# Values for the next image, one step sooner and loaded in fewer transfers

## The chip, the cores and the metric

The kernel runs on one core of a Trainium2 chip. The metric is the device time in microseconds of one execution, the median of several runs. Four compute engines work side by side, each in the order of its own instruction stream: TensorE (PE, matrix products), VectorE (DVE), ScalarE (ACT) and GpSimd (POOL). SyncE (SP) computes nothing here; it issues nearly all DMA transfers, one after the other, and a transfer that has to wait for something holds up every later one of the same stream. Engines wait for each other, and for transfers, through semaphores.

## The reference

The input x is 8 images of 256 channels and 64 x 64 pixels, in float32. Two layers are added to it in turn.

Layer 0 is `x = x + L0(group_norm(x))`: three 1x1 convolutions, a small network that makes a 3x3 kernel for every pixel and group of channels, and the weighted sum of shifted maps with that kernel.

Layer 1 is `x = x + L1(group_norm(x))`, and it is what the change touches. With y the normed map:

```python
q = conv1x1(y, Wq, bq) / 8;  k = conv1x1(y, Wk, bk);  v = conv1x1(y, Wv, bv)      # 4 heads of 64 channels
uk = unfold(pad(k, 3, mode="reflect"), 7);  uv = unfold(pad(v, 3, mode="reflect"), 7)
att = softmax(einsum("bdn,bdkn->bnk", q, uk + position), axis=-1)               # 49 neighbours of each pixel
out_att = einsum("bnk,bdkn->bdn", att, uv)
wts = softmax(einsum("oc,bchw->bohw", Wfc, y) in 9 branches)
out_conv = sum over branches of depthwise3x3(relu(depthwise3x3(y))) * wts
L1 = rate1 * out_att + rate2 * out_conv
```

The point to keep is the reflection: values beyond the edge of the image are copies of rows 1, 2 and 3 (and of columns 1, 2, 3) counted from that edge.

## The kernel before

**Bands and steps.** An image is worked in 8 bands (`NB`) of 8 rows (`R`). Layer 1 of band g is one turn of the main loop, made of 8 steps (`STEPS`): a half of the channels (`ct`) times four pairs of 8 x 8 query tiles (`m`). In the loop's numbering, bands run on over the images: g = 8 b + i for band i of image b. Layer 0 runs 12 bands ahead (`AHEAD`) in the same loop, so its work for the next image lies among the steps of this one. Before g = 0 there are 12 lead-in turns with layer 0 alone, whose steps are much shorter.

**One step.** A step scores a tile pair against its keys (L737), masks and exponentiates (L751, L759, L768), transposes the probabilities of the step before (L774, copied out at L776), multiplies transposed probabilities by values into the tile `small` (L786), and does two products of the dynamic weights, `pf` (L873), evicted by ACT with an exponential (L878). The products with the values are done in the even steps, for the two steps before.

**Who orders what.** The schedule is written out by hand. `beside(g, s)` gives two lists of work that lies beside the attention of step s: `mid` runs in the middle of the step, before its second `pf` product, and `end` at its end. `steer(g, s)`, at the head of a step, issues loads: rows of x for layer 0 (`xc`, `xs`, `xg`), neighbours of layer 0's maps (`x3q`, L389 to L397), and the next band's residual `xr` (L997). `after(n, f)` defers work by n places, six places to a step. The Tile framework adds the semaphores; it never reorders an engine's stream.

**Values.** The padded map of values has 70 rows, cut into 9 chunks of 8 rows: chunk 0 holds three reflected rows and rows 0 to 4; chunk 8 holds the last three true rows and three reflected ones; the chunks between are shifted by three rows against the bands. Each query tile of band i needs chunks i and i + 1. A chunk j is made in three moves:

- `values(b, j, half)` (L592) multiplies normed rows `yp` by `wv` in two halves; ACT copies the results to `vc` (L600), a tile with a single buffer.
- `store_values` sends `vc` to a DRAM buffer `vd` of 8 rows of 70 columns: two transfers for the inner columns (L616), and six, or twelve where the number of rows is odd (chunk 0), for the reflected columns (L621, L625).
- `value_tile(b, j, u)` loads tile u of the chunk, u = 0 to 3, into a buffer `vt` (L642). There are 11 such buffers, reused in turn. For an inner chunk a tile takes two transfers. For chunks 0 and 8 it takes eight: two for the run of true rows and two for each of the three reflected rows, which are read from their source rows.

The rows `yp` of a band are loaded by `load_rows` (L553 to L557) and normed in place on ACT by `normalise` (L562). `pf`, `pv`, `ptp` and other short results share a ring of four PSUM buffers, in the order in which they are asked for.

**The seam between two images.** Chunk i + 2 is made in band i of its own image at steps 4 and 5, stored at the end of step 5 and loaded at the end of step 7. The first two chunks of an image have no such place, so they are made in band 7 of the image before (for image 0, in the last lead-in turn). Chunk 0 is made at steps 4 and 5 and loaded at the end of step 7; chunk 1 is made at steps 6 and 7, stored at the end of step 7, and loaded in band 0 of its own image: tile 0 at the end of step 0, tile 1 at the end of step 1, tiles 2 and 3 at the end of step 2. PE reads the first of them at step 2. Chunk 8 is made at step 4 of band 6 and loaded at the end of its step 7. Rows of `yp` for the next image are loaded at the ends of steps 0 and 1 of band 7 and normed at the ends of steps 1, 2 and 3.

Of the kernel before, what the change touches and what calls it, by code (L numbers as in the profile page):

```python
# [23 lines left out]
R = 8  # L24
BAND = R * W
NB = H // R
# [21 lines left out]
PAD = KA // 2  # L48
WP = W + 2 * PAD
TQ = 8  # L50
# [3 lines left out]
KW = TQ + 2 * PAD  # L54
# [32 lines left out]
def conv_layers_kernel(ctx: ExitStack, tc: tile.TileContext, ins: dict, out: bass.AP):  # L87
    nc = tc.nc
# [121 lines left out]
    images = [Image() for b in range(B)]  # L210
# [348 lines left out]
    def normalise(b, i, ct):  # L559
        im = images[b]  # L560
        v = im.yp[i][:, ct, PAD if i == 0 else 0 : PAD + R if i == NB - 1 else RP]
        nc.scalar.activation(v, v, AF.Identity, bias=im.aff[:, ct, 1:2], scale=im.aff[:, ct, 0:1])  # L562
# [44 lines left out]
    def store_values(b, j):  # L607
# [9 lines left out]
        for d in range(1, PAD + 1):  # L617
            for to, c in ((PAD - d, d), (PAD + W - 1 + d, W - 1 - d)):
# [3 lines left out]
                else:  # L622
                    for p in range(2):
                        o = vd[at + p : at + p + 2 * count[p] - 1 : 2, to : to + 1].rearrange("u c n -> c u n")
                        nc.sync.dma_start(out=o, in_=vc[p * W + c : p * W + c + 1, : count[p]])  # L625

    def value_tile(b, j, u):


        im = images[b]  # L630
        vd = im.vd[j]
        vt = im.vt[j, u] = w1.tile([CHUNK, 2, C], F32, tag="vt", name=f"vt_{b}_{j}_{u}", bufs=11)
        if j == 0:
            runs = [(PAD, PAD, R - PAD)] + [(PAD - d, PAD + d, 1) for d in range(1, PAD + 1)]
        elif j < NB:
            runs = [(0, 0, R)]
        else:
            runs = [(0, 1, PAD)] + [(PAD - 1 + d, PAD - d, 1) for d in range(1, PAD + 1)]
        for to, at, n in runs:
            for g in range(2):  # L640
                c0 = (2 * u + g) * TQ
                nc.sync.dma_start(  # L642
                    out=vt[to * KW : (to + n) * KW, g], in_=vd[at : at + n, c0 : c0 + KW]
                )

    def new_keys(i):

# [3 lines left out]
    def position(b, i):  # L651

        first, last = new_keys(i)
        n, a = last - first, i * R + first
        pe = images[b].pe[i] = w1.tile([P, KW - PAD, W], F32, tag="pe", name=f"pe_{b}_{i}", bufs=1)
        nc.gpsimd.tensor_add(
            pe[:, :n],
            pecol.unsqueeze(1).to_broadcast([P, n, W]),
            perow[:, a : a + n].unsqueeze(2).to_broadcast([P, n, W]),
        )  # L660

    def queries(b, i, ct):

        im = images[b]
        nm = f"{b}_{i}_{ct}"
        kb = im.kb[i, ct] = w1.tile([P, KW, WP], F32, tag="kb", name=f"kb_{nm}", bufs=3)
        if i:
            nc.gpsimd.tensor_copy(kb[:, : 2 * PAD], im.kb[i - 1, ct][:, R:])
        qb = im.qb[i, ct] = w1.tile([P, NT, TQ, TQ], F32, tag="qb", name=f"qb_{nm}")
        pq = ps.tile([P, R, W], F32, tag="gen", name=f"pq_{nm}", bufs=4)  # L670
        for kt in range(NCT):
            nc.tensor.matmul(  # L672
                pq, wq[:, kt, ct * P : (ct + 1) * P], im.yp[i][:, kt, PAD : PAD + R],
                start=(kt == 0), stop=(kt == NCT - 1),
            )
        nc.scalar.activation(
            qb.rearrange("p t r c -> p r t c"), pq.rearrange("p r (t c) -> p r t c", c=TQ),
            AF.Identity, bias=bq[:, ct : ct + 1], scale=HD**-0.5,
        )

    def keys(b, i, ct):


        im = images[b]
        first, last = new_keys(i)
        kb, pe = im.kb[i, ct], im.pe[i]
        bk = chan[:, ct, CBK : CBK + 1]
        pieces = []
        for a in range(first, last, R):
            n = min(R, last - a)  # L690
            pk = ps.tile([P, R, W], F32, tag="gen", name=f"pk_{b}_{i}_{ct}_{a}", bufs=4)
            for kt in range(NCT):
                nc.tensor.matmul(
                    pk[:, :n], wk[:, kt, ct * P : (ct + 1) * P], im.yp[i][:, kt, a : a + n],
                    start=(kt == 0), stop=(kt == NCT - 1),
                )
            pieces.append((a, n, pk))

        def finish():
            for a, n, pk in pieces:  # L700
                nc.vector.scalar_tensor_tensor(
                    kb[:, a : a + n, PAD : PAD + W], pk[:, :n], bk, pe[:, a - first : a - first + n],
                    ALU.add, ALU.add,
                )

                for d in range(1, PAD + 1):
                    src = (W, n), (W - 1 - 2 * d, 2)
                    nc.vector.scalar_tensor_tensor(  # L708
                        strided(kb, a * WP + PAD - d, (WP, n), (W - 1 + 2 * d, 2)), strided(pk, d, *src), bk,
                        strided(pe, (a - first) * W + d, *src), ALU.add, ALU.add,  # L710
                    )
            if i in (0, NB - 1):
                after(2, reflect)

        def reflect():
            for d in range(1, PAD + 1):
                to, at = (PAD - d, PAD + d) if i == 0 else (last - 1 + d, last - 1 - d)
                nc.scalar.copy(kb[:, to], kb[:, at])

        return finish  # L720
# [73 lines left out]
    def small_tile(nm):  # L794

        return ps.tile([P, 4 * P], F32, tag="small", name=f"small_{nm}")
# [117 lines left out]
    def beside(g, s):  # L914

        b, i = divmod(g, NB)
        bn, inx = divmod(g + 1, NB)
        mid, end = [], []

        early = i in (0, NB - 1)  # L920
        if g >= 0:
            if s == 2 - early:
                mid.append(lambda: queries(b, i, 1))
            if s == 3 - early:
                mid.append(lambda: keys(b, i, 1))
        early = inx in (0, NB - 1)
        if 0 <= g + 1 < B * NB:
            if s == 5 - early:
                mid.append(lambda: position(bn, inx))
            if s == 6 - early:  # L930
                mid.append(lambda: queries(bn, inx, 0))
            if s == 7 - early:
                mid.append(lambda: keys(bn, inx, 0))

        made = [(b, i + 2, 4)] if g >= 0 and i < NB - 1 else []
        if i == NB - 1 and 0 <= b + 1 < B:
            made = [(b + 1, 0, 4), (b + 1, 1, 6)]
        for bb, j, d in made:
            if s in (d, d + 1) and (j < NB or s == d):
                mid.append(lambda bb=bb, j=j, d=d: values(bb, j, s - d))  # L940
            if s == d + 1:
                end.append(lambda bb=bb, j=j: store_values(bb, j))
            if s == 7 and d == 4:
                for u in range(NT // 2):
                    end.append(lambda bb=bb, j=j, u=u: value_tile(bb, j, u))
        if g >= 0 and i == 0 and s in (0, 1, 2):
            for u in {0: (0,), 1: (1,), 2: (2, 3)}[s]:
                end.append(lambda u=u: value_tile(b, 1, u))

        nxt = [(b, i + 2, 0)] if g >= 0 and i + 2 < NB else []  # L950
        if i == NB - 1 and 0 <= b + 1 < B:
            nxt = [(b + 1, 0, 0), (b + 1, 1, 1)]
        for bb, ii, d in nxt:
            if s == d:
                end.append(lambda bb=bb, ii=ii: load_rows(bb, ii))
            if s in (d + 1, d + 2):
                end.append(lambda bb=bb, ii=ii, d=d: normalise(bb, ii, s - d - 1))

        alone = g < 0
        if 0 <= g + AHEAD < B * NB:  # L960
            bq_, iq = divmod(g + AHEAD, NB)
            if alone and s == 0:
                mid.append(lambda: small_maps(bq_, iq, small_tile(f"{bq_}_{iq}"))())
            if s == (2 if alone else 0):
                (mid if alone else end).append(lambda: value_maps(bq_, iq, 0))
            if s == (3 if alone else 1):
                mid.append(lambda: value_maps(bq_, iq, 1))
        if 0 <= g + AHEAD - 1 < B * NB and s == (2 if alone else 1):
            bh, ih = divmod(g + AHEAD - 1, NB)

            def hidden():
                parts = hidden_maps(bh, ih, alone)
                if not alone:
                    convs.extend(parts)

            end.append(hidden)
        if 0 <= g + AHEAD - 2 < B * NB and s in TAPS_AT[g < -1]:
            u = TAPS_AT[g < -1].index(s)
            end.append(
                lambda: tap_weights(*divmod(g + AHEAD - 2, NB), u, g < -1, PRODUCTS_AT[g < -1][u])  # L980
            )
        return mid, end
# [24 lines left out]
    with tc.manual_schedule():  # L1007
# [21 lines left out]
        for g in range(-AHEAD, B * NB):  # L1029
            b, i = divmod(g, NB)  # L1030
            for s in range(STEPS):
                ct, m = divmod(s, NT // 2)
                mid, end = beside(g, s)
                steer(g, s)
                if g >= 0:
# [146 lines left out]
```

## Time and profile before

| what | us |
|---|---|
| median of 3 runs (4012.72 to 4017.47) | 4012.74 |
| the profiled execution, as timed | 4010.67 |
| its span in the profile | 4008.9 |
| first scores of image 0 (end of the lead-in) | 246.3 |
| PE busy / DVE / POOL / ACT | 3807.0 / 3419.8 / 3174.8 / 2839.5 |

The page of a profile gives the busy time of each engine, its busy share over the span in 40 slices, and the costliest groups of instructions by line. The wait list says which engine stood still, until what, for how long in total, how many times, and the longest of them. A timeline row has the start, the length, the engine, the line, the operation, the tile written and those read, and in brackets the idle time before it with what ended it. A windows row has the length of a stretch, the busy time of each engine in it, the granted share of the TensorE clock, the busy share of the DMA engines, and the rate. "SPq" is SP's issuing of a transfer, not the transfer.

### The profile page before, as it was taken

The page shows a single profiled execution, that of the slowest core. Times are in us where ns is not written, and L with a number is a line of the kernel's source. Part 1 is how long each engine was busy: PE and PEld are TensorE (multiplying, and loading weights), DVE is VectorE, ACT ScalarE, POOL GpSimd, SP SyncE. Part 2 cuts the span into 40 slices and gives each one's busy share as a digit, 9 for nine tenths or more (in the row PEclk, how much of TensorE's full clock was granted, in tenths as well). Part 3 has the DMA queues.
Part 4 walks back from the last instruction along what each step waited for, and adds up shares of the span by engine and source line. Part 5 has one row for each costly group of instructions (what it writes and reads, how often), then busy time and mean ns, then how long its engine had stood idle before and what let it go on. Part 6 is the DMA issues. An engine that isn't in the chain of part 4 may idle for free.

```text
span 4008.9 us, 72420 instructions
## 1 busy us (share of the span) xinstructions
PE 3807.0 (95%) x24620; PEld 2116.9 (53%) x24620; DVE 3419.8 (85%) x7143; ACT 2839.5 (71%) x6779; POOL 3174.8 (79%) x2156
## 2 busy tenths in 40 slices
PE   6879999999999999999999999999999999999998
PEld 3445555555555555555555555555555555555554
DVE  5868988888888988888988888978988889977888
ACT  3457777677676777777777677777777677676776
POOL 4758988788987988878887888978888888965665
PEclk9989999999999999999999999999999999999999
DMA  8864543544444443444443544444443544322220
GB/s 230 201 165 113 134 114 104 136 125 113 127 115 122 124 124 101 125 132 120 124 115 104 138 125 118 110 130 124 118 115 90 129 116 104 85 61 88 71 65 32
DMA packets 493171, 469.42 MB, mean 117 GB/s; under 512 B 68432, under 2 KB 394624, under 8 KB 492544
## 3 DMA queue, kind: packets, MB, share of 16 engines
q1 hardware_dynamic: 489472, 460.23, 43.4%
q10 hardware_dynamic: 3328, 4.55, 0.3%
q8 instruction: 195, 3.19, 0.3%
q14 instruction: 176, 1.44, 0.1%
HBM read 325.64 MB, written 138.99 MB: 116 GB/s over the span
## 4 chain that ended last, share of the span: by engine, by line
PE 27%; POOL 26%; DVE 22%; ACT 10%; issue 7%; DMA 5%; SPq 3%; POOLq 0%; DVEq 0%; ACTq 0%
PE pf L873 13%; POOL xg L487 13%; POOL ex L1080 6%; DVE prod L479 5%; DVE acc L856 5%; DVE rec L894 4%; PE small L786 3%; ACT x L343 3%; PE sco L737 2%; PE ptp L774 2%; ACT ex L878 2%; DVE prob L751 2%; DMA x3q<-x 2%; PE pq L672 2%; DVE acc L830 2%
## 5 line engine op out<-in xcount | busy, mean ns | idle before, releaser
L873 PE MATMUL pf<-yp,c_wfc 128*128 128x512 f32 x4096 | 1917.1, 597 | 6.2 <-ACT ex L878 5.1
L487 POOL TENSOR_TENSOR xg<-xg,prod 128x1024 f32<-128x1024 f32 x549 | 1200.7, 2187 | 177.2 <-DVE prod L479 148.3
L873 PEld LDWEIGHTS pf<-yp,c_wfc 128*128 128x128 f32 x4096 | 744.0, 191 | 730.3 <-issue 647.1
L1080 POOL TENSOR_TENSOR ex<-ex,ex 128x1024 f32<-128x1024 f32 x384 | 907.9, 2364 | 55.9 <-ACT ex L878 51.8
L479 DVE SCALAR_TENSOR_TENSOR prod<-pw,c_par,x3q 128x1040 f32<-128x1040 f32 x576 | 737.9, 1288 | 124.8 <-PE pw L466 56.1
L830 DVE SCALAR_TENSOR_TENSOR acc<-yp,c_chan,acc 128x504 f32<-128x504 f32 (+3 forms) x1104 | 775.0, 702 | 50.7 <-ACT acc L821 30.3
L856 DVE SCALAR_TENSOR_TENSOR acc<-hid,c_chan,acc 128x504 f32<-128x504 f32 (+3 forms) x1024 | 749.8, 732 | 18.1
L878 ACT ACTIVATE ex<-pf 128x512 f32<-128x512 f32 x1024 | 602.1, 588 | 204.2 <-PE pf L873 184.3
L759 ACT ACTIVATE prob<-prob,nmax 128x196 f32<-128x196 f32 x1024 | 459.2, 451 | 217.1 <-DVE nmax L751 216.9
L768 ACT ACTIVATE prob<-prob,tot 128x196 f32<-128x196 f32 x1024 | 413.0, 452 | 235.3 <-DVE tot L766 235.1
L895 POOL TENSOR_TENSOR tot<-tot,rec 128x256 f32<-128x256 f32 x254 | 185.4, 730 | 412.9 <-DVE rec L894 387.9
L894 DVE RECIPROCAL rec<-tot 128x256 f32<-128x256 f32 x256 | 445.9, 1742 | 17.2 <-POOL tot L889 12.3
L776 ACT COPY pt<-ptp 112x512 f32<-112x512 f32 x511 | 294.8, 577 | 123.4 <-PE ptp L774 122.3
L751 DVE CUSTOM_DVE_ANT_0 prob<-sco,c_mask 128x196 f32<-128x196 f32 x1024 | 324.5, 354 | 20.4 <-PE sco L737 20.2
L786 PE MATMUL small<-pt,vt 112*64 112x64 f32 x8144 | 300.3, 226 | 37.5 <-DMA vt<-vd 37.1
L774 PEld LDWEIGHTS ptp<-ident,prob 128*112 128x112 f32 x2044 | 228.1, 134 | 188.9 <-issue 135.2
L774 PE MATMUL ptp<-ident,prob 128*112 128x128 f32 x2044 | 322.9, 281 | 1.3 <-ACT vc L600 1.3
L786 PEld LDWEIGHTS small<-pt,vt 112*64 112x64 f32 x8144 | 261.5, 138 | 116.7 <-issue 75.4
L737 PE MATMUL sco<-kb,qb 64*64 64x196 f32 x4096 | 236.1, 343 | 39.6 <-DVE kb L708 32.9
L592 PE MATMUL pv<-c_wv,yp 128*128 128x256 f32 (+1 forms) x1056 | 252.8, 382 | 2.6 <-ACT ex L878 2.1
L369 PE MATMUL p<-xc,w3s 128*128 128x512 f32 x512 | 248.4, 609 | 7.0 <-ACT ex L878 7.0
L466 PEld LDWEIGHTS pw<-h2n,c_c 128*128 128x128 f32 x1152 | 173.3, 191 | 153.5 <-issue 113.1
(139 smaller groups left out, 4756.9 us busy)
## 6 DMA issues: line engine op xcount, KB each, us to landing
vt<-vd SPq DMA_DIRECT2D x448, 112.0 KB
x<-x3n SPq DMA_DIRECT2D x128, 264.0 KB
x3q<-x SPq DMA_DIRECT2D x128, 264.0 KB
xc<-in_x SPq DMA_DIRECT2D x64, 512.0 KB
xg<-in_x SPq DMA_DIRECT2D x256, 128.0 KB
x<-xg SPq DMA_DIRECT2D x256, 128.0 KB
yp<-x SPq DMA_DIRECT2D x128, 256.0 KB
xr<-x SPq DMA_DIRECT2D x64, 512.0 KB
```

The lines of the kernel that those rows point to most:

```text
L479: nc.vector.scalar_tensor_tensor(prod[:, :, :RUN], pw[:, j, :RUN].unsqueeze(1).to_broadcast([P, SHARE, RUN]), par[:, PCB2 + k : PCB2 + k + 1],
L487: nc.gpsimd.tensor_add(im.xg[i], im.xg[i], rows(prod))
L759: nc.scalar.activation(prob[:, h, :NKEY], prob[:, h, :NKEY], AF.Exp, bias=nmax[:, h : h + 1], scale=-1.0, accum_out=tot[:, h : h + 1],)
L768: nc.scalar.activation(prob[:, h, :NKEY], prob[:, h, :NKEY], AF.Copy, scale=tot[:, h : h + 1])
L774: nc.tensor.transpose(ptp[:, h, ch], prob[:, h, ch * CHUNK : (ch + 1) * CHUNK], ident)
L786: nc.tensor.matmul(po[half[h], :, t * TQ : (t + 1) * TQ], im.vt[i + ch, m][:n, t, (2 * ct + h) * HD : (2 * ct + h + 1) * HD], pt[:n, h, ch ...
L830: nc.vector.scalar_tensor_tensor(o, yp[:, ct, ra + dr : rb + dr, ca + dc : cb + dc], chan[:, ct, CW1 + k : CW1 + k + 1], o, ALU.mult, ALU.add,
L856: nc.vector.scalar_tensor_tensor(o, hid[:, ra + dr : rb + dr, ca + dc : cb + dc], chan[:, ct, CW2 + k : CW2 + k + 1], o, ALU.mult, ALU.add,)
L873: nc.tensor.matmul(pf, wfc[:, kt, 2 * m + j, ct * P : (ct + 1) * P], images[b].yp[i][:, kt, PAD : PAD + R], start=(kt == 0), stop=(kt == N ...
L878: nc.scalar.activation(ex[:, j].rearrange("p (r c) -> p r c", r=R), pf, AF.Exp)
L894: nc.vector.reciprocal(rec, v)
L1080: after(4, lambda ex=ex, exb=exb: nc.gpsimd.tensor_add(ex, ex, exb))
```

## The change

Three things, in `value_tile`, a new `mirror_rows`, and `beside`:

- The reflected rows of chunks 0 and 8 are written into `vd` itself by three copies from DRAM to DRAM, one step after the chunk's store. A tile of these chunks is then loaded like any other, in two transfers.
- In band 7 (and the last lead-in turn) chunk 0 is made at steps 3 and 4, chunk 1 at steps 5 and 6, each one step sooner, with its store. Chunk 0 is still loaded at the end of step 7.
- Chunk 1's tiles are loaded in the middle of a step: 0 and 1 in step 0 of band 0, 2 and 3 in step 2.

Per image 48 fewer tile loads are issued (120 to 72) and 6 more copies.

```diff
+    def mirror_rows(b, j):
+        vd = images[b].vd[j]
+        for d in range(1, PAD + 1):
+            to, at = (PAD - d, PAD + d) if j == 0 else (PAD + d, PAD - d)
+            nc.sync.dma_start(out=vd[to], in_=vd[at])
+
     def value_tile(b, j, u):
         im = images[b]
         vd = im.vd[j]
         vt = im.vt[j, u] = w1.tile([CHUNK, 2, C], F32, tag="vt", name=f"vt_{b}_{j}_{u}", bufs=11)
-        if j == 0:
-            runs = [(PAD, PAD, R - PAD)] + [(PAD - d, PAD + d, 1) for d in range(1, PAD + 1)]
-        elif j < NB:
-            runs = [(0, 0, R)]
-        else:
-            runs = [(0, 1, PAD)] + [(PAD - 1 + d, PAD - d, 1) for d in range(1, PAD + 1)]
-        for to, at, n in runs:
-            for g in range(2):
-                c0 = (2 * u + g) * TQ
-                nc.sync.dma_start(
-                    out=vt[to * KW : (to + n) * KW, g], in_=vd[at : at + n, c0 : c0 + KW]
-                )
+        at, n = (0, R) if j < NB else (1, 2 * PAD)
+        for g in range(2):
+            c0 = (2 * u + g) * TQ
+            nc.sync.dma_start(out=vt[: n * KW, g], in_=vd[at : at + n, c0 : c0 + KW])
...
         made = [(b, i + 2, 4)] if g >= 0 and i < NB - 1 else []
         if i == NB - 1 and 0 <= b + 1 < B:
-            made = [(b + 1, 0, 4), (b + 1, 1, 6)]
+            made = [(b + 1, 0, 3), (b + 1, 1, 5)]
         for bb, j, d in made:
             if s in (d, d + 1) and (j < NB or s == d):
                 mid.append(lambda bb=bb, j=j, d=d: values(bb, j, s - d))
             if s == d + 1:
                 end.append(lambda bb=bb, j=j: store_values(bb, j))
-            if s == 7 and d == 4:
+            if s == d + 2 and j in (0, NB):
+                end.append(lambda bb=bb, j=j: mirror_rows(bb, j))
+            if s == 7 and j != 1:
                 for u in range(NT // 2):
                     end.append(lambda bb=bb, j=j, u=u: value_tile(bb, j, u))
-        if g >= 0 and i == 0 and s in (0, 1, 2):
-            for u in {0: (0,), 1: (1,), 2: (2, 3)}[s]:
-                end.append(lambda u=u: value_tile(b, 1, u))
+        if g >= 0 and i == 0 and s in (0, 2):
+            for u in (s, s + 1):
+                mid.append(lambda u=u: value_tile(b, 1, u))
```

## The prediction

> **What bounds the kernel now.** I read the page first: busy shares, then the slices.
>
> ```profile
> PE 3807.0 (95%) x24620; PEld 2116.9 (53%) x24620; DVE 3419.8 (85%) x7143; ACT 2839.5 (71%) x6779; POOL 3174.8 (79%) x2156
> PE   6879999999999999999999999999999999999998
> ```
>
> PE is at 9 in every slice after the lead-in, so from the first attention band on (246 us) only two things cost time: PE's work, and what makes PE stop. So the next view is the list of waits, PE's rows of it, and one of ACT's:
>
> ```profile
> PE small L786 <- DMA vt<-vd: 37.1, 15, 8.0
> PE sco L737 <- DVE kb L708: 32.9, 58, 1.3
> ACT vc L600 <- DMA vd<-vc: 16.5, 6, 11.9
> ```
>
> PE's longest wait is for value tiles: 37.1 us in 15 stops. In windows of one image each it comes once per image, in band 0 at step 2: 8.9 us in image 0, then 2.9, 4.1, 4.1, 5.1, 3.5, 2.6 and 5.8 (28.1 in images 1 to 7). The second row is 58 short stops all over the kernel, not near the change. The timelines of PE and of SP's queue show the stop of image 1:
>
> ```profile
> 751.90 0.80 PE L786 MATMUL small<-pt,vt 112*64 112x64 f32 x20
> 755.32 0.55 PE L786 MATMUL small<-pt,vt 112*64 112x64 f32 x8 [2.61 <-DMA vt<-vd]
> 756.17 0.34 PE L786 MATMUL small<-pt,vt 112*64 112x64 f32 x4 [0.30 <-DMA vt<-vd]
> 756.92 3.17 PE L873 MATMUL pf<-yp,c_wfc 128*128 128x512 f32 x4
> ```
> ```profile
> 716.57 1.26 SPq L616 DMA_DIRECT2D vd<-vc  x2
> 717.88 7.87 SPq L625 DMA_DIRECT2D vd<-vc  x12
> ...
> 729.30 17.12 SPq L642 DMA_DIRECT2D vt<-vd  x32
> 746.53 1.33 SPq L616 DMA_DIRECT2D vd<-vc  x2
> 747.90 3.83 SPq L621 DMA_DIRECT2D vd<-vc  x6
> 752.41 1.44 SPq L642 DMA_DIRECT2D vt<-vd  x2
> ```
>
> SP issues back to back for 25 us. The 32 loads of chunk 0 hold it for 17.12 us, chunk 1's store waits behind them to 746.53, its first tile goes out at 752.41 and PE, which asked for it at about 752.3, gets it at 755.3. The transfer is not slow, its issue is late. The stop costs more than its length: four pf matmuls took 3.17 us where the same group takes 1.88. The windows view (next to last: granted clock) says why:
>
> ```profile
> 751.06:770.15 19.09, 15.59 (x90) 8.49 (x89) 13.48 (x30) 10.53 (x25) 12.28 (x8) 0.91 0.52 166
> 757.40:760.70 3.30, 3.30 (x5) 1.27 (x4) 2.25 (x3) 2.38 (x4) 2.19 (x2) 0.50 0.92 323
> ```
>
> After the stop the clock is half for about 3.4 us. And ACT, in the same place, waits for rows of band 2 that SP issued only at 753.93:
>
> ```profile
> 758.32 1.14 ACT L562 ACTIVATE yp<-yp,aff 128x896 f32<-128x896 f32 x1 [5.79 <-DMA yp<-x]
> ```
>
> [...] in seven 19 us stretches, one for each stop of images 1 to 7, the clock is 0.91 (four) or 0.82 (three). [...] the copies wait for the stores, the tile loads for the copies. [...] A reflected row is 70 x 256 floats, 71.7 KB, and in the built program is a 16 x 1120 copy[...]. No trace here shows a DRAM to DRAM copy.
>
> **The change, part by part.**
>
> *Eight loads for 32, three copies.* For chunks 0 and 8 of each image, SP loses 24 issues and gains 3. In the trace 32 loads take 17.12 us; full-height loads take 4.49 us for 6, so 8 take 6.0. Three copies at the 0.5 of a small load are 1.6. Net 9.5 us of SP per chunk. SP time costs nothing by itself; it moves what is behind it. The copies' latency is unseen: from below 1.3 us (last store issued 725.75, ACT released 727.06), from above, if one ran at the 117 GB/s mean of the page, 2 us more each; I take landed 3 us after issue. Step 7 asks for it over 8 us after the copies, so it hides; it would show only beyond some 13 us.
>
> *One step sooner.* Matmuls of values (pv) move from steps 4 to 7 of band 7 to steps 3 to 6. PE's total is the same. At step 3, pv would come to PE at 698.05; its rows' second half is normalised by ACT from 696.97 for about 1 us, so the wait is 0 to 0.3 us. pv (1.72 us) then falls into a stop that PE has there anyway (1.02 us at 700.95, for a PSUM buffer): taken as zero. Steps 6 and 7 lose the 1.72 us, with POOL busy 15.76 of their 15.99 us; POOL's slack is in the next two steps (7.27 of 17.3).
>
> *SP's new order around image 1.* Chunk 0's second copy is out of ACT by about 711.5 (step 4 is at 709.5, and 1.7 later by step 3's longer work). Stores 9.2 us: 720.7. xr and x3q, moved behind them, 5.7: 726.4 (first used after 750). Copies: 728.0. Chunk 1's store 5.2: 733.2. xs and x1, 3.3: 736.5. Eight loads: 742.5. Tiles 0 and 1 of chunk 1, now at mid step 0 (buffers free at 735.7), 3.0: 745.5. Against 752.41 the first of them goes 9.9 us sooner and lands by 747, 5 us before PE asks. Rows of band 2 go at 745.5 in place of 753.93, landing about 750.5; ACT asks at 752.5. So both late transfers are in time; tiles 2 and 3 go at about 753, due at 766.
>
> *What it adds.* vc has one buffer: ACT may write chunk 1 into it only when chunk 0's stores have landed. In the trace ACT waits 0.87 us for that. In the new place stores land at 722.0 and ACT comes at about 717.5, since steps 4 and 5 are shorter than 5 and 6 with their double key matmuls: 4.5 us of wait. Behind it on ACT stand the evictions of pf and ptp. PE can go on while the ring of four PSUM buffers holds: pf of step 6 needs the buffer of this pv, at 722.2, free at 722.5. So 0.3 us is what I can derive, 1 us with what follows on DVE and POOL; bounds 0 and 3.5. Times 7: 7 us.
>
> **The sum.** Images 1 to 6: band 0 lasts 66.8, 69.4, 67.2, 68.8, 67.3, 66.4 us, first scores matmul to first scores matmul, 405.9 in all. Less stop and half clock (1.7 us at 0.91, 3.4 at 0.82) they leave 62.2, 63.6, 61.4, 60.3, 60.4, 62.1: the longer the stop, the more the other engines caught up in it. Without any stop I take 62.2 for all: 405.9 - 373.2 = 32.7. Image 7: 5.8 + 3.4 = 9.2, taken as 8.5. Image 0: SP does the same in short lead-in steps; ACT stands 11.87 us for vc there, store and first scores come 4 to 5 us sooner, and the last needed tile lands at about 265.6 in place of 275.3: 10. Less 7. Together 44. The profiled execution is 4010.7 (span 4008.9), so 3966.5; it is 2 us under the median, so 3968 against 4012.7.
>
> **The rivals.**
> - *All of it comes back*: the vc wait stays inside the ring, and ACT without its 5.8 us wait loses no catching up: 28.1 + 17.0 (clock) + 12 = 57, 3956. For: the 0.3 us above. Against: ACT-ended stops of 0.6 to 1.3 us in bands 7 and 0.
> - *The wait moves*: ACT's 4.5 us reaches PE as 3.5 us and brings its own half clock, 1.7: 5.2 in place of 1 in seven images, 29 us of the 44 lost: 3997.
> - *Slower*: the same vc wait, if SP comes to the stores late. To undo 44 us each image must lose 7.3, 1.7 of it clock, 5.6 idle; with the ring's 4 that is an ACT wait of 10 us, stores starting 6 us after 711.5. With 8 us more it is 4030. For: image 0's 11.87. Against: SP is idle from 704.3 in the trace.
> - *Nothing*: another late transfer takes the place of the tiles (rows of band 2 have 2 us, xs about 2.5): PE stops as before, 4008.
>
> **How the numbers follow.** Forecast 0.68, all 0.12, moved 0.11, slower 0.05, nothing 0.04. The range 3950 to 3998 takes in the first three with the vc bounds (0 to 3.5 us). 0.2% (8 us) is about what a measurement of this kernel can tell. Faster 0.90, same 0.04, slower 0.06.
>
> **What would show it.** Right: no wait of PE for vt in images 1 to 7, clock 1.00 in band 0, band 0 at 61 to 63 us, SP's run of L642 at step 7 about 6 us, ACT's wait for vc at 3 to 5 us per image, band 7 at 63 to 65. Wrong: PE still waiting for vt (SP not freed), pv waiting for yp at step 3, or pf waiting for ACT over 2 us in band 7.

## The result and the profile after

| | before | after |
|---|---|---|
| median, us | 4012.73 (4 runs, 4010.49 to 4017.47) | 3962.82 (4 runs, 3955.92 to 3964.21) |
| the profiled execution, timed / its span | 4010.67 / 4008.9 | 3964.1 / 3962.3 |

The ratio is 0.9869 [0.9854, 0.9885]: faster by 49.9 us, where 44 were forecast. The page after opens with nearly the same busy times; what went is PE's stopping, not its work:

```profile
PE 3794.8 (96%) x24620; PEld 2110.4 (53%) x24620; DVE 3418.4 (86%) x7143; ACT 2839.8 (72%) x6779; POOL 3174.4 (80%) x2156
```

The list of waits after, PE's line for value tiles and ACT's two for transfers (us in total, times, longest):

```profile
PE small L785 <- DMA vt<-vd: 1.7, 2, 1.3
```
```profile
ACT vc L600 <- DMA vd<-vc: 24.0, 6, 7.4
ACT yp L562 <- DMA yp<-x: 10.8, 4, 5.7
```

PE's 37.1 us for tiles are down to two stops in image 0. ACT's wait for rows (`yp`) is down from 63.7 us to 10.8. The wait that the change adds, for `vc`, is there: the list has it up from 16.5 to 24.0, and image by image it is 3.2 to 5.0 us ahead of images 1 to 7 (for two of them the profile names PE as what ended it). PE's timeline at step 2 of band 0 of image 1, after:

```profile
752.66 1.15 PE L785 MATMUL small<-pt,vt 112*64 112x64 f32 x32
...
754.23 1.88 PE L872 MATMUL pf<-yp,c_wfc 128*128 128x512 f32 x4
```

The 32 products run in one piece, and `pf` behind them takes 1.88 us in place of 3.17. The windows view of the same 19 us stretch has the clock (the third number from the end) at full speed:

```profile
751.06:770.15 19.09, 18.85 (x165) 11.28 (x164) 16.80 (x37) 13.20 (x30) 16.87 (x10) 1.00 0.55 167
```

SP's timeline over the same seam (each row a run of issues of one line):

```profile
711.19 1.29 SPq L616 DMA_DIRECT2D vd<-vc  x2
712.53 7.88 SPq L625 DMA_DIRECT2D vd<-vc  x12
...
724.81 2.11 SPq L632 DMA_DIRECT2D vd<-vd  x3
729.96 1.30 SPq L616 DMA_DIRECT2D vd<-vc  x2
731.30 4.14 SPq L621 DMA_DIRECT2D vd<-vc  x6
...
738.75 8.85 SPq L643 DMA_DIRECT2D vt<-vd  x12
747.70 0.40 SPq L553 DMA_DIRECT2D yp<-x  x1
```

The 12 loads at 738.75 are eight of chunk 0 and four of chunk 1. At 0.74 us each, the first tile of chunk 1 goes out at about 744.7 (forecast 742.5; before, 752.41), and PE asks for it at about 753.3. The rows of band 2 go at 747.70 (forecast 745.5; before, 753.93). ACT, after:

```profile
721.79 0.59 ACT L600 COPY vc<-pv 128x512 f32<-128x512 f32 x1 [3.46 <-DMA vd<-vc]
...
753.21 1.12 ACT L562 ACTIVATE yp<-yp,aff 128x896 f32<-128x896 f32 x1
```

The new wait is 3.46 us; the old one for rows (5.79 us) is gone.

**Where the time came from.** Bands are measured as in the prediction, first scores to first scores; "image 0" runs from the last small maps of the lead-in (L328) to band 1.

| stretch | before, us | after, us | difference | forecast |
|---|---|---|---|---|
| lead-in, to its last small maps | 212.8 | 216.8 | +4.0 | |
| image 0 | 106.2 | 103.1 | -3.0 | -10 |
| band 0 of images 1 to 6 | 67.64 on average | 61.03 | -39.7 in all | -32.7 |
| band 0 of image 7 | 58.50 | 50.25 | -8.2 | -8.5 |
| band 7 of images 0 to 5 (the vc wait) | 63.46 on average | 63.54 | +0.5 in all | +7 over seven images |

These add up to 46.4 of the 46.6 us by which the spans differ. The other 24 loads saved per image, those of chunk 8 at the end of band 6, bought nothing: bands 1 to 6 take 2734.8 us in all before and 2734.7 after, and band 7, which uses chunk 8, is no shorter. No reordering by the change explains the lead-in's part: the two traces drift apart by 2 us and more from about 130 us on, and every engine does the same work in the same order in both until 218. The place lies between 212 and 217 us in the twelve kernels run here. The two that keep the 32 loads have the two lowest values; why stays open.

### The profile page after: what moved, and what is told of

It reads as the page before. It is cut to its first block, busy times and chain, and to the rows that moved or that the text cites. A ratio compares the mean times of both kernels' runs of the same rounds, so it can differ in the third digit from the quotient of the medians.

```text
span 3962.3 us, 71885 instructions
## 1 busy us (share of the span) xinstructions
PE 3794.8 (96%) x24620; PEld 2110.4 (53%) x24620; DVE 3418.4 (86%) x7143; ACT 2839.8 (72%) x6779; POOL 3174.4 (80%) x2156
## 4 chain that ended last, share of the span: by engine, by line
PE 33%; POOL 26%; DVE 19%; ACT 9%; issue 6%; DMA 4%; SPq 3%; POOLq 0%; DVEq 0%; ACTq 0%
PE pf L872 15%; POOL xg L487 13%; POOL ex L1081 6%; DVE prod L479 4%; DVE rec L893 4%; DVE acc L855 4%; PE small L785 3%; ACT x L343 3%; PE sco L736 3%; PE ptp L773 2%; PE pq L671 2%; PE pk L692 2%; ACT ex L877 2%; POOL tot L888 2%; PE pv L592 2%
## 5 line engine op out<-in xcount | busy, mean ns | idle before, releaser
L736 PE MATMUL sco<-kb,qb 64*64 64x196 f32 x4096 | 235.9, 343 | 35.5 <-DVE kb L707 32.7
L888 POOL TENSOR_SCALAR tot<-tot 128x512 f32<-128x512 f32 x127 | 243.6, 1918 | 11.1
```

## The experiments

Four kernels make a square of the fewer loads and the earlier step. The third part of the change, the place of chunk 1's loads within a step, is the old one in both kernels that leave something out; E7 tests it.

| | old steps | one step sooner |
|---|---|---|
| 32 loads of chunk 0 | 4012.7 (before) | 4033.3 (E2) |
| 8 loads and 3 copies | 3958.2 (E1) | 3962.8 (after) |

**E1, fewer loads alone** (edit against the changed kernel):

```diff
-            made = [(b + 1, 0, 3), (b + 1, 1, 5)]
+            made = [(b + 1, 0, 4), (b + 1, 1, 6)]
...
-        if g >= 0 and i == 0 and s in (0, 2):
-            for u in (s, s + 1):
-                mid.append(lambda u=u: value_tile(b, 1, u))
+        if g >= 0 and i == 0 and s in (0, 1, 2):
+            for u in {0: (0,), 1: (1,), 2: (2, 3)}[s]:
+                end.append(lambda u=u: value_tile(b, 1, u))
```

> Only the reflected-row copies and the eight loads; values made at steps 4 to 7 as before, and chunk 1's tiles loaded at the ends of steps 0, 1 and 2 as before. Theory 1 (SP's 17 us of issues at step 7 made the tiles late): SP ends chunk 0's loads near 738 us instead of 746.4 around image 1, chunk 1's first tile goes at about 743 to 745 and lands by 748, before PE asks at 752. So no stop in images 1 to 7, band 0 at 61 to 62 us, and 3960 to 3968 in all: all of the gain from this part. ACT's wait for vc stays under 1 us. Rival (the step sooner is what brings the tiles in time): chunk 1 is stored too late without it, PE still waits 2 us or more per image with its half clock, and the time is 3990 to 4010.

Measured: 3958.21 us (4 runs, 3956.64 to 3960.37), just below the 3960 to 3968 expected; ratio to before 0.9865 [0.9849, 0.9882]. On SP's timeline of this kernel the loads of chunk 0 and the first tile of chunk 1 are

```profile
726.30 5.75 SPq L643 DMA_DIRECT2D vt<-vd  x8
...
738.22 1.41 SPq L643 DMA_DIRECT2D vt<-vd  x2
```

and PE, which comes to the products at 745.59 in this run, doesn't stop (it does in image 0, for 1.9 us). Band 0 of images 1 to 6 is 61.36 us, at full clock. So the whole gain comes with the fewer loads. The earlier step adds 0.33 us per image (61.36 to 61.03), 2 us over six images, and loses more than that in image 0, whose band 0 is 64.6 us here and 68.3 in the changed kernel.

What the 32 loads held up was SP, not the DMA engines. The windows view of the kernel before, over the 17.1 us in which it issues them, has the DMA engines busy for a share of 0.26 (the last number but one):

```profile
729.30:746.40 17.10, 16.34 (x101) 9.08 (x100) 13.54 (x36) 13.46 (x35) 10.91 (x10) 1.00 0.26 73
```

**E2, one step sooner alone** (against the kernel before):

```diff
-            made = [(b + 1, 0, 4), (b + 1, 1, 6)]
+            made = [(b + 1, 0, 3), (b + 1, 1, 5)]
...
-            if s == 7 and d == 4:
+            if s == 7 and j != 1:
```

> Only the step sooner for chunks 0 and 1, with their stores; 32 loads for chunks 0 and 8 and chunk 1's tiles at the ends of steps 0, 1 and 2, as before. Theory 1: SP does the same issues, with xr, x3q and now chunk 1's store (5 us) ahead of the 32 loads, so these end near 756 us around image 1 instead of 746.4 and the first tile of chunk 1 lands at 759: PE stops 6 to 8 us per image, the clock is half for 3.4 to 6.8 us after it, band 0 at 70 to 72 us, 4035 to 4060 in all. Rival (the step sooner brings the tiles in time): PE's stop shrinks or goes and the time is 3965 to 4000.

Measured: 4033.34 us (4 runs, 4032.48 to 4038.01), ratio 1.0054 [1.0039, 1.0069]: slower, if by a little less than the 4035 to 4060 expected. SP's timeline and PE's around image 1:

```profile
743.53 18.42 SPq L642 DMA_DIRECT2D vt<-vd  x34
```
```profile
763.52 1.27 PE L786 MATMUL small<-pt,vt 112*64 112x64 f32 x12 [6.03 <-DMA vt<-vd]
764.73 1.10 PE L774 MATMUL ptp<-ident,prob 128*112 128x128 f32 x4
765.62 3.62 PE L873 MATMUL pf<-yp,c_wfc 128*128 128x512 f32 x4
```

Chunk 1's store now stands ahead of the 32 loads on SP and waits for its values, so the loads begin at 743.53 in place of 729.30. Its first tile, the last two of these 34 issues, goes out at about 760.5 (before, 752.41). PE stops for 6 us, the clock is at 0.50 for 10.2 us around it, and band 0 of images 1 to 6 is 69.8 us on average.

**E3 and E8, the loads of chunk 0 issued three times and twice** in the changed kernel, into the same tiles (the values are the same, and SP's time grows). The loads of `value_tile` are split off as `load_tile`; E3 adds the lines below behind the first loads, E8 the same with `for u in range(NT // 2)`:

```diff
+                if j == 0:
+                    for u in 2 * list(range(NT // 2)):
+                        end.append(lambda bb=bb, u=u: load_tile(bb, 0, u))
```

> The changed kernel, with chunk 0's eight loads issued three times over (16 more issues at the end of step 7, about 11.5 us of SP). Theory 1: the slack of about 5 us that the tiles of chunk 1 have is used up, the first of them goes near 756 us around image 1 and lands at 758.5, so PE stops 5 to 7 us at step 2 of band 0, then runs 3.4 or 6.8 us at half clock; band 0 at 68 to 72 us, 4012 to 4045 in all. The half clock's price is read from it: 1.7 or 3.4 us beside the stop. Rival (transfers, not issues, set the time): 1.8 MB more per image would show as a busy share of the DMA engines near 1 and late rows everywhere; otherwise under 10 us in all.

> The changed kernel, with chunk 0's eight loads issued twice (8 more issues, about 5.8 us of SP). Theory: chunk 1's first tile goes near 750.5 us around image 1 and lands by 753, as PE asks: the slack is just used up, stop of 0 to 1 us per image, no half clock, band 0 at 61 to 62.5 us; rows of band 2 come 3 to 5 us late to ACT. Rival (slack smaller than 5 us): stops of 2 us or more, half clock, band 0 over 64 us.

Measured: E3 4042.35 us (4 runs, 4041.47 to 4042.83), ratio 1.0074 [1.0059, 1.0089], band 0 of images 1 to 6 71.0 us. E8, one execution: 3999.26 us, band 0 65.5 us. E8's PE and ACT around image 1:

```profile
757.20 1.09 PE L789 MATMUL small<-pt,vt 112*64 112x64 f32 x12 [1.82 <-DMA vt<-vd]
```
```profile
761.16 1.13 ACT L562 ACTIVATE yp<-yp,aff 128x896 f32<-128x896 f32 x1 [5.97 <-DMA yp<-x]
```

Nothing but more loads brings all of the old loss back, and more. The rival named for E3, that transfers and not their issue set the time, would have the DMA engines near full: while SP issues E3's 28 loads (745.9 to 765.6) their share is 0.51. Eight more loads are some 5.7 us; PE stopped for 1.2 on average, so tiles had about 4.5 us to spare (forecast 5). But band 0 is 4.5 us longer than 61.0, with stops for tiles of 1.2, where 61 to 62.5 were expected; and half clock, of which none was expected, follows in images 1, 3 and 7. More is at work than tiles. The second row shows a candidate: rows of band 2 come late too.

**E6, copies as late as possible**, at step 7 just ahead of the loads that read them:

```diff
-            if s == d + 2 and j in (0, NB):
+            if s == 7 and j in (0, NB):
```

> The changed kernel, with the three DRAM to DRAM copies issued at the end of step 7, right ahead of the tile loads that read them, instead of one step after the store. The gap on SP between the last copy and the first tile load is the copy's landing time. Theory: 1.5 to 3 us, so tiles go out 2 to 4 us later than in the changed kernel, inside their slack of about 5 us: bands 0 stay at 61 to 61.5 us. Rival (a copy is slow, 8 us or more): PE stops for vt at step 2 of band 0 and band 0 is over 64 us.

Measured, one execution: 3978.01 us, band 0 63.9 us where 61 to 61.5 were expected. SP, ACT and PE around image 1:

```profile
734.99 1.87 SPq L632 DMA_DIRECT2D vd<-vd  x3
738.68 8.66 SPq L643 DMA_DIRECT2D vt<-vd  x12
747.45 0.40 SPq L553 DMA_DIRECT2D yp<-x  x1
```
```profile
753.06 1.13 ACT L562 ACTIVATE yp<-yp,aff 128x896 f32<-128x896 f32 x1 [4.58 <-DMA vt<-vd]
```
```profile
755.42 1.98 PE L872 MATMUL pf<-yp,c_wfc 128*128 128x512 f32 x4 [0.86 <-ACT pt L775]
...
764.25 0.72 PE L466 MATMUL pw<-h2n,c_c 128*128 128x132 f32 x4 [1.43 <-ACT ex L877]
```

From the end of the last copy's issue (736.86) to the first load is 1.82 us of waiting: that is all that the copies' landing takes there, below the 3 us assumed. Tiles are just in time (0.46 us of stop in image 1, 0.92 in image 6, none in images 2 to 5), but the rows are late. ACT waits 4.58 us for what it norms (the profile names another load of the same queue), and PE then waits for ACT, 2.2 us per image more than in the changed kernel. No half clock shows in images 1 to 7.

**E9 and E10, late tiles with the rows in time.** Tiles 0 and 1 of chunk 1 are loaded behind the rows, at the end of step 1; E10 loads tile 1 first, `{1: (1, 0), 2: (2, 3)}`:

```diff
-        if g >= 0 and i == 0 and s in (0, 2):
-            for u in (s, s + 1):
-                mid.append(lambda u=u: value_tile(b, 1, u))
+        if g >= 0 and i == 0 and s in (1, 2):
+            for u in {1: (0, 1), 2: (2, 3)}[s]:
+                end.append(lambda u=u: value_tile(b, 1, u))
```

> The changed kernel with tiles 0 and 1 of chunk 1 loaded at the end of step 1 of band 0, behind the rows of band 2: now only tiles are late, the rows are not. Around image 1 the first of them should go out at about 751.7 us, land at 755, and PE, which asks at about 753.3, should stop for some 1.8 us, as with chunk 0 loaded twice (1.82). Theory, late tiles and late rows of band 2 cost separately: a stop for tiles costs its own length, and 1.7 more where half clock follows. Band 0 of images 1 to 6 then lasts 62.8 to 64.5 us against 61.0, and the kernel about 3977 to 3988 us. Rival, late rows cost nothing and a stop for tiles costs more than its length and clock: band 0 at 65.5, as with chunk 0 loaded twice, and about 3996 us.

> As the run before it, with tile 1 loaded ahead of tile 0, so that the tile which PE asks for first goes out 1.4 us later: a stop of about 3.2 us, about that of the kernel before (2.9), with rows of band 2 in time. Theory, late tiles and late rows cost separately: 61.0 + 3.2 + 1.7 for half clock = 65.9 us for band 0, about 3998 us in all. Rival, late rows cost nothing: band 0 as in the kernel before, 67.6 us, and about 4010 us.

Measured, one execution each: 3974.42 us and 3988.29 us; band 0 of images 1 to 6 is 62.3 and 64.5 us. E9's SP and PE around image 1, and E10's PE:

```profile
746.24 0.39 SPq L553 DMA_DIRECT2D yp<-x  x1
...
752.21 5.69 SPq L643 DMA_DIRECT2D vt<-vd  x8
```
```profile
755.27 0.45 PE L785 MATMUL small<-pt,vt 112*64 112x64 f32 x8 [0.43 <-DMA vt<-vd]
755.93 0.34 PE L785 MATMUL small<-pt,vt 112*64 112x64 f32 x4 [0.21 <-DMA vt<-vd]
```
```profile
755.51 1.06 PE L785 MATMUL small<-pt,vt 112*64 112x64 f32 x12 [2.15 <-DMA vt<-vd]
756.50 1.10 PE L773 MATMUL ptp<-ident,prob 128*112 128x128 f32 x4
757.39 2.60 PE L872 MATMUL pf<-yp,c_wfc 128*128 128x512 f32 x4
```

The stops came out at 0.8 and 2.4 us on average, less than the 1.8 and 3.2 expected, so both times are below the expectation. The theory's sum holds and the rival's doesn't: in images 1 to 7 ACT had no wait for rows, and the band grew by the stop and its half clock alone, to 0.33 us or less. E8 has stops between these two and is longer than both.

The six band-0 stretches of each kernel put side by side, as averages in us. "Other stops" are PE's waits for ACT and DVE, less those of the changed kernel (1.76); half clock is counted at half its length, an estimate from the granted share of 0.50. "Sum" is 61.03 and the three columns.

| kernel | tile stops | other stops | half clock | sum | measured |
|---|---|---|---|---|---|
| after | 0 | 0 | 0 | 61.03 | 61.03 |
| before | 3.73 | 0.61 | 2.27 | 67.64 | 67.64 |
| E9 tiles late | 0.80 | 0.11 | 0 | 61.94 | 62.27 |
| E10 tiles later | 2.40 | -0.12 | 1.13 | 64.44 | 64.51 |
| E6 rows late | 0.23 | 2.16 | 0 | 63.42 | 63.88 |
| E8 both late | 1.18 | 2.00 | 0.57 | 64.78 | 65.51 |

So late rows cost 2 to 3 us through ACT where PE hardly stops for tiles (E6). In the kernel before ACT waited longer for them, 5.4 to 8.4 us in images 1 to 6 against 2.5 to 4.6 in E6, and yet PE's other stops were only 0.6 us longer. The reading that fits is that PE stood still for tiles, or ran at half clock, while ACT caught up: the stop for tiles hid the late rows.

**E7, tiles of chunk 1 loaded in mid step, old steps.** Against the changed kernel only the `made` line goes back, as in E1.

> The loads-only kernel, with chunk 1's tiles loaded in the middle of steps 0 and 2 as in the changed kernel; values at steps 4 to 7. Theory: the place of these loads does nothing once SP is free, so band 0 of images 1 to 6 stays at 61.3 to 61.4 us. Rival (the middle of the step gives the last 0.3 us of band 0): 61.0.

Measured, one execution: 3966.01 us, band 0 of images 1 to 6 61.41 us (E1: 61.36). The place in the step does nothing there.

**E4 and E5, image 0.** In the changed kernel image 0 gained 3 us where 10 were forecast. PE's timeline after, in the last lead-in turn; DVE's and PE's in band 0:

```profile
228.63 1.22 PE L592 MATMUL pv<-c_wv,yp 128*128 128x256 f32 x2 [5.65 <-ACT yp L562]
```
```profile
265.30 1.29 DVE L283 BATCH_NORM_STATS2 st<-xs 128x6 f32<-128x512 f32 x2 [8.33 <-DMA xs<-in_x]
```
```profile
269.84 3.37 PE L872 MATMUL pf<-yp,c_wfc 128*128 128x512 f32 x4 [3.30 <-ACT ex L877]
```

`pv`, one short step sooner, comes before its rows are normed; and `xs`, issued behind chunk 1's store at 261.62 (before, 244.07), holds DVE for 8.33 us, then ACT, then PE. E4 issues `xs` earlier at each seam:

```diff
-        if s == (3 if g < -1 else 7) and g + AHEAD0 < B * NB:
-            first_stats(*divmod(g + AHEAD0, NB), n=40 if g < -1 else 9)
+        seam = g >= -1 and i == NB - 1
+        if s == (3 if g < -1 else 4 if seam else 7) and g + AHEAD0 < B * NB:
+            first_stats(*divmod(g + AHEAD0, NB), n=40 if g < -1 else 27 if seam else 9)
```

> The changed kernel, with the load of xs in band 7 and the last lead-in turn issued at step 4 instead of step 7 (its statistics stay in place). Theory 2 (image 0 gained nothing because xs, now behind chunk 1's store on SP, came 8.3 us late to DVE, which held ACT's exponentials and PE for 3.3 us and brought half clock): DVE's wait for xs goes, PE's 3.3 us stop for pf at step 0 of image 0 goes, 4 to 6 us off: 3956 to 3960, with images 1 to 7 unchanged (61.0 us). Rival (image 0's loss is the order of pv on PE in the lead-in, or chance there): xs in time moves DVE's wait to something else, under 2 us.

Measured: 3959.52 us (4 runs, 3957.1 to 3962.45), ratio 0.9868 [0.9853, 0.9883]; images 1 to 7 unchanged. The wait for `xs` is gone, and PE's timeline has another in its place:

```profile
268.08 1.11 PE L785 MATMUL small<-pt,vt 112*64 112x64 f32 x12 [4.16 <-DMA vt<-vd]
```

Band 0 of image 0 is 67.2 us against 68.3. The total came in as expected, but not by the expected way: 1.1 us went in that band, as the rival had it (under 2), and 2.7 in the lead-in turn before it, which varies by more than that. E5 keeps the old steps and loads for image 0 and the new ones for the others:

```diff
-            made = [(b + 1, 0, 3), (b + 1, 1, 5)]
+            made = [(b + 1, 0, 3), (b + 1, 1, 5)] if b + 1 else [(0, 0, 4), (0, 1, 6)]
...
-        if g >= 0 and i == 0 and s in (0, 2):
+        if g == 0 and s in (0, 1, 2):
+            for u in {0: (0,), 1: (1,), 2: (2, 3)}[s]:
+                end.append(lambda u=u: value_tile(b, 1, u))
+        if g > 0 and i == 0 and s in (0, 2):
```

> The changed kernel, but for image 0, whose chunks keep the steps and load places they had before the change (with the copies and eight loads). Theory: from the last lead-in turn's small maps to band 1 of image 0 it takes the 97 us of the loads-only kernel (not the 103 of the changed one), and from there to the end the 3642 of the changed one (not 3643.5): 3953 to 3959 in all, since the lead-in before it varies by some us. Rival (image 0 in the changed kernel was slow by chance): still 101 us or more for image 0.

Measured: 3960.58 us (4 runs, 3956.94 to 3965.56), ratio 0.9867 [0.9851, 0.9884]. Band 0 of image 0 is 64.3 us, near E1's 64.6. But the expectation was missed: from the last small maps to band 1 it took 100.6 us, not 97. The lead-in turn took 36.3 us where E1's took 32.6, in the same order of work, and that ate the difference: no total can be told from E1's or the changed kernel's. What makes that turn vary (29.8 to 36.9 us over the kernels run) stays open. E1 is the shorter edit for the same time.

## Why the prediction was right, step by step

**The bound and its cause: right.** SP's late issue made PE stop, and half clock followed. Of the 6.61 us that band 0 lost per image, the table gives 3.73 to the stop and 2.27 to half clock, both priced in the prediction. E1 (SP freed, nothing else), E3 and E8 (SP filled again) and E2 (the queue made longer) all move the time in the direction that this chain says.

**The order of SP: right within 2 to 3 us.** Chunk 0's store was forecast for 711.5 and came at 711.19; copies were to end at 728.0 and ended at 726.92. The bound on a copy, "2 us more each" at 117 GB/s, doesn't come out of its numbers: 71.7 KB at that rate are 0.6 us, some 2 us for all three, and in E6 SP waited 1.82 us after the last issue. The sum did not rest on it. Chunk 1's store ended 2.2 us later than worked out, because SP stood idle for 3.0 us (726.92 to 729.96) for the second half of its values. Both late transfers followed: the tiles still had some 5 us, the rows hardly any. ACT came to them at 753.21, 2.7 us after the last of them went out (750.49); in E8 ACT was released 2.2 us after that.

**Images 1 to 6: mis-sized, -32.7 for -39.7.** The step that failed is the floor of 62.2 us. The six remainders, stop and half clock taken off, average 61.7; the first of them was taken, with the argument that other engines catch up during a longer stop. The other 0.6 is the table's second column for the kernel before: PE's stops through ACT, which by E6 late rows bring. The prediction saw the rows as a wait and gave them no price.

**The new wait: mis-sized, +7 for +0.5.** ACT's wait was there, 3.46 us in image 1 for 4.5 forecast, but it did not reach PE, which has no stop for ACT there: the ring of four PSUM buffers held. Band 7 is 63.54 us against 63.46. The rival "all of it comes back" was right on this step; of the two that let it reach PE next to nothing is seen.

**Image 0: mis-sized, -10 for -3.0.** "SP does the same in short lead-in steps" holds for the loads: E1's band 0 of image 0 is 8.1 us shorter than before. It fails for the earlier step, with which 3.7 of these are lost again, to `xs`, which the prediction had named as tight, and with `xs` in time (E4) to tiles behind it. That the total came so close is in part luck. The miss of the new wait and that of image 0 nearly cancel; the floor's 7 us, less the lead-in's 4, make the difference between 44 and 46.6. The rest up to 49.9 is the spread of the runs: the profiled execution was among the slower of its four.

**One step sooner: no part of the gain.** Its matmuls were priced at nothing on PE, and band 7 agrees (0.08 us longer). But the prediction counted it towards the earlier issue. The square shows that alone it costs 20 us, and with fewer loads it makes no difference that these runs can tell.

## What to carry to other kernels

Where one queue issues nearly everything, count its issues and not bytes alone: here 32 small loads held SP for 17.12 us with the DMA engines busy for a share of 0.26. With 24 fewer per chunk the kernel took 3958.2 us in place of 4012.7 (E1). The earlier start by itself made things worse (4033.3 us, E2), by putting a waiting store ahead of the loads, which began at 743.53 in place of 729.30. When two transfers are late at one place, price each with the other in time, as E9, E10 and E6 do: the stop for tiles hid most of the late rows' price here, and by E6 curing the tiles alone would have left 2 to 3 us per image.

## What the hardware showed that was not expected

- Stops of like length did not cost alike in half clock. In the traces of the kernels before and after, from the first scores to the last products, the changes of the clock lie whole multiples of 3.413 us apart, and half clock lasted one to three such stretches. The stop of 2.15 us around image 1 in E10 left PE idle for 2.08 us of one stretch, and the next ran at half clock. Around image 3 PE was idle for 2.86 us in all over two stretches, and the one behind them ran at full clock. The rows are two stretches of image 1 and three of image 3:

```profile
752.02:755.43 3.41, 1.33 (x36) 0.88 (x28) 1.65 (x5) 2.88 (x4) 2.19 (x1) 1.00 0.46 140
755.44:758.84 3.40, 3.33 (x18) 2.38 (x19) 2.22 (x4) 1.20 (x4) 0.26 (x1) 0.50 0.42 128
1711.16:1714.57 3.41, 2.02 (x40) 1.41 (x39) 1.86 (x5) 3.36 (x5) 1.76 (x2) 1.00 0.52 169
1714.58:1717.98 3.40, 1.93 (x18) 1.39 (x19) 1.09 (x3) 0.69 (x3) 0.61 (x1) 1.00 0.48 145
1717.99:1721.40 3.41, 3.41 (x12) 1.84 (x11) 3.37 (x5) 2.82 (x9) 2.55 (x2) 1.00 0.07 26
```

PE is idle for 2.08 us of the first row, and for 1.39 and 1.47 us of the third and fourth. In the traces of the kernels before and after, over the same part, nine stretches at full clock were followed by one at half, each with 1.61 us of idle PE or more; those followed by full clock had 1.43 us at most. In E8 (image 3) PE was idle for 1.41 us between 1716 and 1720 us, in short stops, and half clock followed. So the price of a stop in half clock could not be told here from its length alone.
- A DRAM to DRAM copy of 71.7 KB was complete within 1.82 us of the end of its issue around image 1 in E6; SP's longest wait for such copies in that run was 2.7 us.
- The lead-in, with the same order of work in twelve kernels, took 212.2 to 216.9 us to its last small maps. In the changed kernel a band takes the same time in images 1 to 5 to within 0.1 us, with one exception (0.3 us), so an effect below 0.1% of the total can be read there and not from totals.
